# Attention's output projection: seven block products for a pair of tiles, weights loaded in pieces, page numbers read from on-chip memory

## The chip, the cores and the metric

The kernel runs on one core of one Trainium2 chip. Its time is device microseconds (us) of one execution, and the median of several runs is given. The engines that appear below are TensorE (PE; its weight loads are shown apart as PEld), VectorE (DVE), ScalarE (ACT), GpSimd (POOL) and SyncE (SP). Each engine runs its own instructions in order and waits for others through semaphores. SP computes nothing here: it issues almost all DMAs. POOL issues the gathers.

## What is computed

Four layers, each a "condition" stage and a feed-forward stage with a residual, over 64 sequences of 32 tokens with 512 features (2048 rows). The change lies in the condition stage of layer 2, paged attention:

```python
q = rope(rmsnorm(x @ Wq.T))            # 32 heads of 128
k = rope(rmsnorm(x @ Wk.T)); v = x @ Wv.T   # 8 heads of 128
kc = k_cache[block_table].reshape(bsz, L, HK, D)   # 16 pages of 32 keys a sequence
vc = v_cache[block_table].reshape(bsz, L, HK, D)
scores = einsum('bqhd,bkhd->bhqk', q, concat(kc, k)) * SCALE   # masked by cache_seqlens
o = einsum('bhqk,bkhd->bqhd', softmax(scores), concat(vc, v))
return einsum('bse,de->bsd', o.reshape(bsz, seqlen, HQ * D), Wo)   # 4096 -> 512
```

The last line, the product with Wo, is what is computed in another way. Everything is float32.

## The kernel before

The 2048 rows are 16 tiles of 128 rows (four sequences each). Layers 0 and 1 run first, then `attention`, then the `Tail` (layer 2's feed-forward and layer 3).

Attention goes through `steps`: two halves of the heads (16 query heads and 4 key heads each), and in each half the 16 tiles, so 32 steps. A step has 16 turns (4 sequences x 4 key heads). A turn transposes the probabilities of its own scores (L635, `prT_ps`), starts the scores of two turns later (L791 on PE, then L796 to L803 on DVE and ACT) and multiplies values (L640, `po`). Between these, each turn has two places for other work, its "slots" (32 in a step): the projections of the next step (`Projection.product`, in halves of 2 matmuls: `pv`, `pk`, `pq`), their transposes (`turned`), loads and stores, and the output product of the step before (`Output.product`). The order of all PE work is written out by hand and kept by `on_pe`.

The output product of one tile in one half is 16 matmuls, one a head, of a 128x128 block of `oT` (the tile's attention output, heads by rows, transposed) with 128x512 of `wo`, accumulated in one PSUM bank (`py`, L640). A float32 matmul stands in the trace as two instructions, so 32 steps x 16 heads give the 1024 instructions of the profile. `wo` is one resident tile of 16x512 floats a partition, loaded in four DMAs of 1 MB at the start of each half (L855). The first half's result goes to DRAM (`y_part`, L774), the second's is added to it (L770) and stored as `y`. The output of the last step has no turns left to lie between: it runs alone at the end of attention, before the tail.

On SP's queue, `load_keys` loads a sequence's 16 key pages as 16 DMAs of 64 KB (L98). Before them `numbers` (L93) reads the 16 page numbers from DRAM into registers of SP, and checks each against bounds. The tile of keys has two buffers (`cp`), so a load waits until PE is done with the scores of the sequence two before. The values are gathered by POOL (L662). POOL also does two operations of each rotation (L694, L695) and its inverse root (L126), which PE's transposes of q and k need. SP, POOL, DVE and ACT each go through their queues in order: what stands behind a waiting instruction waits too.

## Time and profile before

| | |
|---|---|
| median of 3 runs | 3710.6 us (3705.92 to 3713.36) |
| the profiled execution, its own time | 3681.84 us |
| its span, first to last instruction | 3679.8 us |
| PE busy | 3631.7 us (99%) |
| DVE, ACT, POOL busy | 1805.6, 1316.3, 1254.1 us |
| DMA moved | 407.70 MB, mean 111 GB/s |
| granted TensorE clock | 0.999 |

A group's line gives its engine, operation, what it writes and reads, its shape and count, then the busy time and the mean duration of one. Matmuls overlap in the pipeline: one lasts longer than the distance to the next. The distance between starts, read from the timeline, is what a matmul costs a PE that never idles.

### The profile page before, as it was taken

How to read it: one execution, taken by the hardware profiler on the slowest of the kernel's cores; microseconds unless marked ns; L12 is line 12 of the kernel's file. 1: busy time of each engine (PE TensorE's matmuls, PEld its weight loads, DVE VectorE, ACT ScalarE, POOL GpSimd, SP SyncE). 2: the span in 40 equal slices, each digit the busy share in tenths (PEclk: the TensorE clock that was granted, in tenths of full speed). 3: DMA queues.
4: the chain of work that ended last, by engine and by line, in shares of the span. 5: the costliest groups of instructions: out<-in, count | busy, mean ns of one | idle time of the engine just before them, and what ended most of it. 6: DMA issues, size and time to landing. Idle time of an engine off the chain costs nothing.

```text
span 3679.8 us, 62184 instructions
## 1 busy us (share of the span) xinstructions
PE 3631.7 (99%) x18752; PEld 2523.7 (69%) x18752; DVE 1805.6 (49%) x4815; ACT 1316.3 (36%) x3014; POOL 1254.1 (34%) x1265
## 2 busy tenths in 40 slices
PE   8999999999999999999999999999999999999999
PEld 3444788888867776777777776777777777777755
DVE  5452222222236655565556655566555655566423
ACT  1111111111125444444444444444444444444411
POOL 0112100000035444544445444444444444454222
PEclk9999999999999999999999999999999999999999
DMA  5014211111144444344443355544444344444521
GB/s 209 23 35 162 92 44 60 44 47 34 37 141 134 124 122 122 117 116 116 123 122 118 115 184 179 165 132 119 123 123 125 117 123 122 129 120 123 160 68 61
DMA packets 410062, 407.70 MB, mean 111 GB/s; under 512 B 49954, under 2 KB 322338, under 8 KB 409730
## 3 DMA queue, kind: packets, MB, share of 16 engines
q1 hardware_dynamic: 363010, 251.65, 22.5%
q0 software_dynamic: 44416, 147.88, 13.2%
q10 hardware_dynamic: 2304, 4.20, 0.3%
q8 instruction: 153, 2.51, 0.3%
q14 instruction: 179, 1.47, 0.1%
HBM read 382.57 MB, written 20.97 MB: 110 GB/s over the span
## 4 chain that ended last, share of the span: by engine, by line
PE 89%; SPq 1%; DMA 0%; DVE 0%; issue 0%; ACT 0%; POOL 0%; ACTq 0%; POOLq 0%; DVEq 0%
PE po L640 14%; PE sc L791 13%; PE pq L640 12%; PE py L640 12%; PE gate_up L311 10%; PE prT_ps L635 6%; PE pz L311 5%; PE po L1100 3%; PE pv L640 3%; PE pk L640 3%; PE po L311 2%; PE qkT_ps L635 2%; PE pd L247 1%; PE ph L122 1%; SPq L93 0%
## 5 line engine op out<-in xcount | busy, mean ns | idle before, releaser
L662 POOL DMA_INDIRECT vt<-in_v_rows,v_rows x512 | 500.7, 978 | 816.7 <-PE po L640 708.8
L640 PEld LDWEIGHTS po<-prT,vt 128*128 128x128 f32 x4096 | 530.1, 192 | 183.7 <-issue 178.0
L796 DVE CUSTOM_DVE_ANT_0 pr<-sc,mask 128x544 f32<-128x544 f32 x512 | 369.2, 721 | 458.7 <-PE sc L791 457.5
L798 ACT ACTIVATE pr<-pr,low 128x544 f32<-128x544 f32 x512 | 383.4, 749 | 540.7 <-DVE low L796 536.4
L791 PE MATMUL sc<-kt,qT 128*128 128x288 f32 (+1 forms) x2048 | 555.1, 394 | 5.2 <-ACT qT L748 2.4
L640 PE MATMUL po<-prT,vt 128*128 128x128 f32 x4096 | 540.8, 275 | 1.6 <-ACT prT L809 1.6
L791 PEld LDWEIGHTS sc<-kt,qT 128*128 128x128 f32 x2048 | 369.2, 191 | 180.8 <-issue 106.9
L640 PE MATMUL py<-wo,oT 128*128 128x512 f32 x1024 | 480.3, 593 | 0.7 <-ACT oT L839 0.7
L640 PE MATMUL pq<-wq,xT 128*128 128x512 f32 x1024 | 480.9, 593 | 0.0
L809 ACT COPY prT<-prT_ps 128x512 f32<-128x512 f32 x512 | 298.5, 583 | 272.6 <-PE prT_ps L635 269.4
L803 DVE TENSOR_SCALAR pr<-pr,low 128x512 f32<-128x512 f32 x512 | 364.5, 712 | 16.7
L635 PE MATMUL prT_ps<-ident,pr 128*128 128x128 f32 x2048 | 310.9, 275 | 1.3 <-DVE pr L803 1.3
L640 PEld LDWEIGHTS py<-wo,oT 128*128 128x128 f32 x1024 | 192.6, 191 | 137.5 <-issue 125.6
L640 PEld LDWEIGHTS pq<-wq,xT 128*128 128x128 f32 x1024 | 182.8, 191 | 129.9 <-issue 125.1
L800 DVE RECIPROCAL low<-low 128x1 f32<-128x1 f32 x512 | 83.5, 163 | 360.6 <-ACT pr L798 359.6
L635 PEld LDWEIGHTS prT_ps<-ident,pr 128*128 128x128 f32 x2048 | 237.7, 141 | 9.1 <-issue 1.5
L126 POOL TENSOR_TENSOR rs<-rs,minus_half 128x4 f32<-128x4 f32 x160 | 166.2, 1039 | 167.4 <-DVE rs L678 166.1
L694 POOL TENSOR_TENSOR rot<-rot,swapped 128x512 f32<-128x512 f32 x160 | 202.7, 1267 | 1.0
L801 ACT ACTIVATE own_pr<-pr,low 128x32 f32<-128x32 f32 x512 | 164.2, 321 | 106.3 <-DVE low L800 104.2
L695 POOL TENSOR_TENSOR rot<-rot,rs 128x512 f32<-128x512 f32 x160 | 177.1, 1107 | 8.0
L395 DVE TENSOR_TENSOR sg<-sg,gate_up 128x256 f32<-128x256 f32 (+1 forms) x88 | 37.1, 421 | 277.3 <-ACT sg L394 277.3
L677 DVE TENSOR_REDUCE rs<-squares 128x4 f32<-128x512 f32 x160 | 109.6, 685 | 118.9 <-ACT squares L675 116.3
(208 smaller groups left out, 4649.8 us busy)
## 6 DMA issues: line engine op xcount, KB each, us to landing
kt<-in_kT SPq DMA_DIRECT2D x2048, 64.0 KB
xt<-x SPq DMA_DIRECT2D x48, 256.0 KB
wq<-in_WqT SPq DMA_DIRECT2D x12, 1024.0 KB
A<-in_A SPq DMA_DIRECT2D x64, 152.0 KB
sets<-in_cond0T SPq DMA_DIRECT2D x32, 256.0 KB
vt<-in_v_rows,v_rows POOLq DMA_INDIRECT x512, 3.7
wo<-in_WoT SPq DMA_DIRECT2D x8, 1024.0 KB
y<-y SPq DMA_DIRECT2D x32, 256.0 KB
```

The lines of the kernel that those rows point to most:

```text
L126: self.nc.gpsimd.tensor_tensor(t, t, self.minus_half[:, :n], ALU.pow)
L311: c.on_pe(nc.tensor.matmul(out, lhsT, rhs, start=start, stop=stop))
L635: c.on_pe(nc.tensor.transpose(pt[:, m, :], piece, c.ident))
L640: c.on_pe(nc.tensor.matmul(out, lhsT, rhs, start=first and i == 0, stop=last and i == len(pairs) - 1))
L662: nc.gpsimd.indirect_dma_start(out=vts[b % 2][:, n, :], out_offset=None, in_=a["v_rows"], in_offset=bass.IndirectOffsetOnAxis(ap=rows[h][: ...
L694: nc.gpsimd.tensor_tensor(r, r, tmp, ALU.add)
L695: last = nc.gpsimd.tensor_tensor(r, r, rs.unsqueeze(2).to_broadcast([P, REP, HD]), ALU.mult)
L791: c.on_pe(nc.tensor.matmul(sc[:, lo + n * PSIZE:lo + m * PSIZE].rearrange("p (n k) -> p n k", k=PSIZE), q, kt[:, n:m, g, :], start=True, s ...
L796: nc.vector.tensor_tensor_reduce(pr[:, :NK], sc[:, lo:lo + NK], masks[h, b], -SCALE, 3.0e38, ALU.add, ALU.min, low[:, 0:1])
L798: nc.scalar.activation(pr[:, :NK], pr[:, :NK], AF.Exp, bias=low[:, 0:1], scale=-1.0, accum_out=low[:, 1:2])
L803: nc.vector.tensor_scalar(pr[:, :L], pr[:, :L], low[:, 2:3], None, ALU.mult)
L809: nc.scalar.copy(prT, pt)
```

## The change

The output of two tiles (steps 2n and 2n+1, the "pair" n) in one half is now one product of a 256x2048 matrix with a 2048x512 matrix. It is cut into 2x2 blocks (rows: the two tiles; inner: the first 8 and the last 8 heads; columns: the first and the last 256), and computed as seven products of blocks in place of eight, with sums of blocks before and after (Winograd's form of Strassen's method):

- `first_sums` (on POOL, for the last pair on DVE) and `next_sum` (DVE) add and subtract blocks of `oT`, partly in place, partly in a new tile `o_sum`. `oT` has three buffers, not two.
- `sum_up` makes the four sums of blocks of Wo, once for each half: 16 times in steps 0 and 1 it loads two 256 KB pieces of Wo, makes four 128x256 sums on DVE, and stores 512 KB to a new DRAM tensor `wo_sums`.
- Each block product is 8 matmuls (one a head) with 256 columns, in two halves of 4. `wo` is no longer resident: a piece of 512 KB (4 heads x 256 columns, rows of 1 KB), from Wo or from `wo_sums`, is loaded for each half product, with four buffers. The next piece is issued by SP one slot after a half product.
- Results are put together by ACT (copies of products 1 and 5), DVE (adds from PSUM) and POOL (two adds of 256 columns; in the second half two adds of `y_before`).
- The slots of projections and outputs are laid out anew for even and odd steps. A pair's 14 half products take 8 slots in the next even step and 6 in the next odd one; the last pair's 14 run alone at the end.
- The page numbers are loaded once into an on-chip tile `pages`, held between the bounds by DVE, and SP reads them from there, without checks.
- All of `load_by`'s DMAs (key pages, wo pieces, sums) are issued in the order of the text. A sequence's 16 page loads are given out in four parts: the first where it was, the others in the next slots, at most two such items a slot.

The core of the diff:

```diff
     def load_by(self, dst, src):
-        self.last_load = self.nc.sync.dma_start(dst, src).ins
+        with self.tc.issue_after(self.last_load) if self.last_load else nullcontext():
+            self.last_load = self.nc.sync.dma_start(dst, src).ins
...
+        def load_keys(h, b, parts=range(4)):
+            if 0 in parts:
+                pages[:] = c.numbers(
+                    known.pages[b:b + 1, :], PAGES,
+                    skip_runtime_bounds_check_because="Known holds them between the bounds")
+            for n in range(parts[0] * NPP // 4, (parts[-1] + 1) * NPP // 4):
+                c.load_by(kts[h, b][:, n, :], a["kT"][ds(pages[n], 1), h].rearrange("a d f -> (a d) f"))
...
+        H = D // 2
+        KH = HQP // 2
+        QH = KH // 2
+        ORDER = (1, 2, 5, 6, 7, 3, 4)
+        ahead = 4
+        def wo_tile():
+            return op.tile([P, QH, H], F32, name="wo", bufs=ahead)
+        def sum_up(h, k):
+            w, t = [], []
+            def rows():
+                w.append(wo_tile())
+                for n in range(2):
+                    at = (h * HQP + n * KH + k) * HD
+                    c.load_by(w[0][:, 2 * n:2 * n + 2, :].rearrange("p a b -> p (a b)"),
+                              a["WoT"][at:at + HD, :])
+            def add():
+                t.append(wo_tile())
+                (b11, b12, b21, b22), (t1, t2, t3, t4) = ([v[0][:, n, :] for n in range(4)] for v in (w, t))
+                nc.vector.tensor_tensor(t1, b12, b11, ALU.subtract)
...
+            def store():
+                c.load_by(sums[h][:, k], t[0])
...
+            def first_sums(self, engine):
+                self.o = [oTs.pop(2 * self.n + i) for i in range(2)]
+                (_, _), (o21, o22) = self.blocks = [(o[:, :KH, :], o[:, KH:, :]) for o in self.o]
+                self.s = qp.tile([P, KH, P], F32, name="o_sum", bufs=1)
+                engine.tensor_tensor(self.s, o21, o22, ALU.add)
+                engine.tensor_tensor(o21, self.blocks[0][0], o21, ALU.subtract)
...
+            def product(self, i):
+                m, u = ORDER[i // 2], i % 2
...
+                    self.acc = ps.tile([P, D], F32, tag="mm", bufs=2, name="py")[:, :H]
+                (o11, o12), (o13, o22) = self.blocks
+                lhs = {1: o11, 2: o12, 3: self.s, 4: o22, 5: self.s, 6: self.s, 7: o13}[m]
+                w = wos.pop(0)
+                part(self.acc, [(lhs[:, u * QH + n, :], w[:, n, :]) for n in range(QH)], u == 0, u == 1)
...
-                load_keys(h, b)
+                load_keys(h, b, range(1))
+                later.extend(partial(load_keys, h, b, range(n, n + 1)) for n in range(1, 4))
...
+                    ats = (18, 19, 21, 23, 25, 27, 29, 31) + tuple(2 * per + at for at in (1, 2, 4, 5, 7, 8))
...
+                        slots[at].append(partial(out.product, i))
+                        slots[at].append(partial(later.append, next_wo))
...
+        out = outputs[-1]
+        out.befores()
+        out.first_sums(nc.vector)
+        for i in range(n_out):
+            out.product(i)
+            next_wo()
+            if i in (5, 7):
+                for u in range(2):
+                    out.next_sum(6 if i == 5 else 3, u)
```

## The prediction

> **What bounds the kernel now.** I read the page's busy table and chain of waits first, to see whether one engine sets the end.

> ```profile
> span 3679.8 us, 62184 instructions
> PE 3631.7 (99%) x18752; PEld 2523.7 (69%) x18752; DVE 1805.6 (49%) x4815; ACT 1316.3 (36%) x3014; POOL 1254.1 (34%) x1265
> PEclk9999999999999999999999999999999999999999
> PE 89%; SPq 1%; DMA 0%; DVE 0%; issue 0%; ACT 0%; POOL 0%; ACTq 0%; POOLq 0%; DVEq 0%
> ```

> PE is busy 99% of the span at full granted clock, and 89% of the chain that ended last is PE's. So time follows what PE must do, unless a change makes PE wait. A busy PE may still hold bubbles, so next I read its timeline for the distance between starts, once in attention, once in layer 1, and at the end of attention.

> ```profile
> 2042.42 1.88 PE L640 MATMUL py<-wo,oT 128*128 128x512 f32 x4
> 2044.14 1.05 PE L640 MATMUL po<-prT,vt 128*128 128x128 f32 x8
> ...
> 900.46 1.89 PE L311 MATMUL gate_up<-xT,gate1T 128*128 128x256 f32 x8
> 902.19 0.60 PE L311 MATMUL gate_up<-low_x,Bg 128*128 128x256 f32 x2
> 902.62 1.89 PE L311 MATMUL gate_up<-xT,up1T 128*128 128x256 f32 x8
> ...
> 3495.25 14.00 PE L640 MATMUL py<-wo,oT 128*128 128x512 f32 x32 [0.67 <-ACT oT L839]
> 3510.03 0.66 PE L1117 MATMUL yT_ps<-ident,y 128*128 128x128 f32 x4 [0.79 <-DVE y L770]
> ```

> Columns: start, length, line, what, count, wait before. Four `py` of 512 columns take 2044.14 - 2042.42 = 1.72 us, 0.430 us each. Ten matmuls of 256 columns in layer 1 take 902.62 - 900.46 = 2.16 us, 0.216 us each: half the columns, half the distance. The last two lines show one output alone at the end, with small waits at both sides.

> Then PE's waits inside attention (from 1081 us to 3495 us), SP's waits, and the stretches of attention with most DMA:

> ```profile
> PE sc L791 <- ACT qT L748: 2.4, 3, 1.0
> PE sc L791 <- DMA kt<-in_kT: 1.6, 1, 1.6
> ...
> SPq L98 <- PE sc L791: 215.0, 72, 5.2
> ...
> 1081.80:1160.00 78.20, 74.08 (x410) 54.08 (x411) 52.13 (x134) 39.48 (x94) 49.41 (x54) 1.00 0.57 175
> 1160.00:1238.00 78.00, 78.00 (x412) 55.30 (x411) 45.73 (x120) 37.18 (x86) 34.59 (x36) 1.00 0.46 133
> 2178.00:2255.00 77.00, 76.96 (x400) 53.97 (x399) 45.31 (x120) 35.55 (x82) 34.89 (x36) 1.00 0.60 194
> 2255.00:2333.00 78.00, 76.27 (x397) 53.52 (x397) 44.34 (x117) 35.55 (x82) 34.36 (x36) 1.00 0.52 162
> ```

> PE waits 8.1 us in all of attention (six kinds, the two longest shown). SP waits 215 us for PE before loads of keys: the queue is early, not late. In the stretches the columns are length, PE, PEld, DVE, ACT and POOL busy, clock, DMA share, GB/s. Even at 194 GB/s and a share of 0.60 PE is busy 76.96 of 77 us; the next stretch loses 1.7 us.

> **The change part by part.**

> *Fewer products (PE).* Before: 32 steps x 16 heads x 2 instructions = 1024 x 0.430 = 440.3 us. After: 32 tile-halves make 16 pairs; each has 7 products x 8 heads x 2 = 112 instructions of 256 columns, 1792 x 0.216 = 387.1 us. All lies on the bounding engine: **-53.2 us**. Weight loads rise from 1024 to 1792; `py`'s last 191 ns each, under the 216 ns between matmuls, and layer 1's `gate_up` loads weights for each of its matmuls too at that pace. Cost 0. The scores' 256-column form would give the same price.

> [...]

> *Sums of Wo in steps 0 and 1.* 16 x 4 = 64 subtractions of 256 columns on DVE at 0.42 us (layer 1's 128x256 tensor-tensor): 27 us in about 151 us (a step is (3495.25 - 1081.77)/32 = 75.4 us). DVE is busy 52 of 78 us and 46 of 78 there, so it rises to about 0.8: hidden by DVE's idle time, but a sum that waits for its rows holds the softmax of a later turn behind it, and PE needs that two turns (9.4 us) on. DMA: 16 x (0.52 + 0.52) = 16.8 MB more, less the 4.2 MB of resident `wo`. Step 0 goes from 175 to about 175 + 111 - 54 = 232 GB/s, step 1 from 133 to 244. With 194 GB/s at share 0.60 (323 GB/s if full), that is a share of 0.72 to 0.76. No row shows attention at this rate. Lower bound 0, indeed -1.6 us (the wait for `kt` could go). Upper: both steps lose what the 162 GB/s stretch lost, scaled by extra traffic to some 8 us a step, 15 us. It is nearest to the 194 GB/s row, which lost nothing: **+2 us**.

> *Pieces of Wo.* 14 a pair, 7.3 MB in 151 us: +49 GB/s, so 129 becomes about 178, below the 194 of the row above; SP pays 7 more issues a step at about 0.52 us (16 key pages take 8.3 us). A piece waits on SP until PE has finished the half product four before. Behind it on SP stand key pages, `xt`, stores; for these wait the scores. But the piece is issued a slot after that product was due, and is needed some 8 slots (8 x 2.36 = 19 us) later. If SP's lead were gone, keys would be next late. SP also gets time back: a sequence's page numbers cost it loads of 0.86 and 1.82 us and 16 checks of 0.17 us, 5.4 us, against one load on chip; a lead that was not needed, so worth 0 to 1.6 us. The page loads in parts come up to two slots later, 4.7 us, against SP's wait of 3.0 us a time and five turns until use. Value 0, bounds -1.6 and +8 (PE's present waits in attention doubled).

> *Sums and adds of outputs.* DVE per pair: before 2 x 0.69, after 5 x 0.42 + 4 x 0.69, +3.5 us in 151; ACT two copies more. POOL: two sums of 1024 columns, by L694's 1.27 us for 512 some 5 us together, and up to 3.8 us of adds. POOL waits for `oT`'s last copies; behind it stand gathers and the rotations that PE transposes five slots (11.8 us) after the projection. DVE idles 42%, POOL 55%: hidden. If it were not, each pair would lose at most the excess of a late rotation, say half a microsecond (PE waits for ACT or DVE today are 0.3 to 1.0 us each), 8 us. Value **+1 us**.

> *The end.* The last pair's 14 half products run alone: 112 x 0.216 = 24.2 us, counted above. The wait of 0.67 for `oT` goes, since product 1 reads the earlier tile. A new one comes between products 5 and 6, where `o_sum` is changed in place: one DVE operation of 512 columns, 0.69 + 0.1, like the 0.79 of the timeline: **+0.1 us** net. Four pieces are there, ten follow at one a 1.73 us: 303 GB/s. Neither the 209 GB/s of the page's first slice nor 323 settles it: 5.24 MB at 209 GB/s take 25.1 us against 17.3, so 0 to 7.8 us. I take **+2 us**, nearer to 323, as the queue then carries little else.

> [...] The profile shows no landing time for 512 KB. [...]

> *Sum.* -53.2 + 2 + 0 + 1 + 0.1 + 2 = **-48.1 us**. The profiled execution took 3681.84 (2.0 around its span), so it would take 3633.7. The median shown is 28.8 us above the profiled one; I carry that over whole: 3710.6 - 48.1 = **3662.5 us**.

> **The rivals.**

> *A: the gain is half eaten by transfers.* All upper bounds come true: steps 0 and 1 15, pieces 8, sums 8, end 7.8: -53.2 + 38.8 = -14.4, 3696; with half of them, 3677. For it: 0.52 and 0.60 shares already cost 1.7 us. Against: SP's 215 us of lead. I set it at 3690.

> *B: slower, by late pieces.* Place: SP's queue, where a piece stands behind key pages that wait for PE up to 5.2 us, and four buffers. If the piece comes after its product is due, PE waits at each of 224 half products. It decides from 53.2/224 = 0.24 us a piece; with the 0.4 us in the middle of PE's present waits it is 90 us, 3747. Against: 19 us of distance; 194 GB/s without loss.

> *C: it does not do what it says.* At 0.246 us a matmul (as the scores' 288-column form has: four `sc` in 0.92 us, less two at 0.216) 1792 cost as much as 1024 did: 3710. Against: every 256-column row has 0.216.

> **How the numbers follow.** Forecast 75%, A 12%, B 9%, C 4%. The forecast alone spans -55 to -40 us and some 4 us between runs: 3652 to 3675. The range reaches through most of A: 3650 to 3697. 0.2% (7.4 us) is about what a measurement can tell from no change. Faster: 0.75 + 0.12 = 0.87; within: C, 0.04; slower: B, 0.09.

> **What would show it.** `py` in 1792 instructions of 256 columns 0.216 us apart; PE still 98 to 99% busy, in a span near 3632; waits of PE for `wo` near 0 before the end and a few us there; steps 0 and 1 near 230 to 245 GB/s with PE full; SP still waiting for PE. Wrong: PE waits for `wo`, `kt` or `rot` in the tens of us, or another distance between `py`.

## The result: slower, by 1.4% in the first comparison

| comparison | kernel before, us | changed kernel, us | ratio, 95% interval |
|---|---|---|---|
| the first | 3711.98 (3705.92 to 3714.83, 4 runs) | 3764.08 (3757.46 to 3768.67, 4 runs) | 1.0141 [1.0119, 1.0163] |
| second, run e5 | 3684.26 | 3698.01 | 1.0033 [1.0019, 1.0048] |
| third, run e11 | 3680.34 | 3700.97 | 1.0051 [1.0034, 1.0068] |
| fourth, run e13 | 3712.72 | 3765.45 | 1.0140 [1.0122, 1.0157] |

The comparisons are of two kinds whatever the kernel: in some the kernel before takes about 3711 us, in others about 3682, and the profile of before that the prediction read (3681.84 us) is of the second kind, while the timed runs shown with it are of the first. I call them the 3711 and the 3682 comparisons. The prediction was 48 us faster, so about 100 us have to be found in the first kind and 62 to 69 in the second.

The page of the changed kernel's first profile (3760.5 us for the execution): the span, the busy times, the granted clock, and the shares of the chain that ended last.

```profile
span 3758.7 us, 60219 instructions
PE 3618.2 (96%) x19520; PEld 2678.1 (71%) x19520; DVE 1896.8 (50%) x4996; ACT 1307.7 (35%) x3046; POOL 1377.4 (37%) x1343
PEclk9999999999999999999999999999999999999999
PE 84%; DMA 4%; POOL 4%; issue 2%; DVE 2%; SPq 1%; ACT 1%; another core or an unknown queue 1%; DVEq 0%; ACTq 0%; POOLq 0%
```

PE is busy 13.5 us less than before (3631.7), where 53 less were forecast, and it idles 140 us of the span in place of 48. Part of what it is busy longer is clock: the mean over the span is 0.990, against 0.999, too fine for the line in tenths. The clock's records show 15 stretches at half speed, 12 of them in attention; the profile of before had 3, none of them there. What PE waits for:

```profile
PE po L652 <- ACT prT L905: 51.4, 17, 3.5
PE qkT_ps L647 <- POOL rot L711: 14.0, 15, 1.1
...
PE sc L887 <- DVE low L892: 7.4, 5, 4.6
PE pk L652 <- DMA wk<-in_WkT: 6.8, 1, 6.8
...
PE py L652 <- DMA wo<-wo_sums: 4.0, 3, 1.7
PE pq L652 <- DMA wq<-in_WqT: 3.6, 1, 3.6
```

And the longest of the waits of SP's queue:

```profile
SPq L100 <- PE sc L887: 764.4, 118, 12.1
```

None of the waits is the one that rival B named: `py` waits 4.0 us for pieces of `wo` in all. SP waits 764 us for PE before loads of keys (215 before), so its lead has grown. The longest wait, 51.4 us, is for ACT's copy of `prT`, 17 times at up to 3.5 us; 13 of them, 44.6 us, stand at the first turn of a pair of steps, and two more such turns wait 2.7 and 2.0 us with "issue" as the cause. Before the change all of attention had 8.1 us of waits.

To see where the time goes I cut attention into its 16 pairs of steps, by the starts of the first transposes of `prT` in the timeline (the last pair reaches to the first `yT_ps`). "Forecast" is the kernel before (run e15) with what the products alone move: 13.74 us out of pair 0, 3.29 out of each other pair, and 7.16 into the last.

| pairs, us | before, e15 | forecast | after, first | after, e5 | best, e10 |
|---|---|---|---|---|---|
| 0 (steps 0, 1) | 143.6 | 129.8 | 151.3 | 149.3 | 141.0 |
| 1 to 6, 8 to 14, each | 151.66 | 148.37 | 152.8 to 157.0 | 150.2 to 151.0 | 149.0 to 149.4 |
| 7 (change of halves) | 153.4 | 150.1 | 169.9 | 171.2 | 149.0 |
| 15 and the last output | 151.9 | 159.1 | 169.3 | 165.0 | 161.6 |

Over the forecast the first profile loses 21.5 us in pair 0, 82.7 in the 13 steady pairs, 19.8 at the change of halves and 10.2 at the end. In e5 the same four are 19.5, 24.8, 21.1 and 5.9: three lie within 5 us of the first profile's, and the steady pairs are what differs between the two kinds of comparison.

### The profile page after: what moved, and what is told of

Read it like the earlier page. It is cut to its first block, busy times and chain, and to the rows that moved or that the text cites. A ratio compares the mean times of both kernels' runs of the same rounds, so it can differ in the third digit from the quotient of the medians.

```text
span 3758.7 us, 60219 instructions
## 1 busy us (share of the span) xinstructions
PE 3618.2 (96%) x19520; PEld 2678.1 (71%) x19520; DVE 1896.8 (50%) x4996; ACT 1307.7 (35%) x3046; POOL 1377.4 (37%) x1343
## 4 chain that ended last, share of the span: by engine, by line
PE 84%; DMA 4%; POOL 4%; issue 2%; DVE 2%; SPq 1%; ACT 1%; another core or an unknown queue 1%; DVEq 0%; ACTq 0%; POOLq 0%
PE po L652 13%; PE sc L887 10%; PE gate_up L313 10%; PE pq L652 10%; PE py L652 10%; PE prT_ps L647 5%; PE pz L313 4%; PE po L1237 3%; PE ph L124 3%; PE pk L652 2%; PE pd L249 2%; PE pv L652 2%; PE po L313 2%; PE qkT_ps L647 2%; DMA wo<-in_WoT 1%
## 5 line engine op out<-in xcount | busy, mean ns | idle before, releaser
L652 PE MATMUL po<-prT,vt 128*128 128x128 f32 x4096 | 553.3, 279 | 57.5 <-ACT prT L905 51.4
L652 PE MATMUL py<-wo,oT 128*128 128x256 f32 x1024 | 241.9, 380 | 4.0 <-DMA wo<-wo_sums 4.0
L652 PE MATMUL py<-wo,o_sum 128*128 128x256 f32 x768 | 181.0, 379 | 0.1
```

Of the source, the lines that this page charges most:

```text
L652: c.on_pe(nc.tensor.matmul(out, lhsT, rhs, start=first and i == 0, stop=last and i == len(pairs) - 1))
```

## The experiments

Each kernel is the changed one with the edit shown, unless another is named. Each was timed beside the kernel before.

### Is it the program or the occasion?

Five runs without an edit: the kernel before (e1, e15) and the changed one (e5, e11, e13).

> The kernel before, unchanged, profiled once more. Its first profile (3681.84 us, clock 0.999) lies 29 us under its timed runs (3705.92 to 3713.36); the changed kernel's profile (3760.5) lies among its timed runs. Theory: an execution of the kernel before takes about 3710 us as a rule and loses the 29 us to stretches of granted clock below 1.0 that the first profile did not catch: this profile then shows a span near 3705 and a clock near 0.992. Rival: the profile of before is always near 3682 and only unprofiled executions are longer: span 3680, clock 0.999.

> The changed kernel, unchanged, once more. The wait for ACT's copy of prT (51.4 us in its first profile) is 1.9 us or less in three variants of it, of which two (page numbers from DRAM, first sums on DVE) don't touch the work between scores and values at the turn where it stood. Theory 1 (it belongs to this program's order): the wait is here again, 45 to 55 us with a clock near 0.990, and the time stands 1.2 to 1.6% over the kernel before. Theory 3 (it belongs to the execution of that day, as the 29 us of the kernel before did): the wait is under 10 us, the clock 0.995 or more, the time within 0.3% of the variant with the first sums on DVE, 0.2 to 0.8% over the kernel before.

> The changed kernel, unchanged, a third time, to see on which chips the wait of 51.4 us for ACT's copy of prT stands. Where the kernel before takes about 3684 us I expect what the last run of it showed: steady pairs of 150.2 us, a wait for prT under 2 us, 1.0033 of the kernel before. Where the kernel before takes about 3710 us I expect the wait of 51 us, steady pairs of 153.5 to 156.5 us and 1.014.

Measured: e1 3681.64 us, 0.9996 [0.9987, 1.0006] of the runs beside it, span 3688.8, clock 0.997. Neither theory's numbers; the kernel before simply takes 3682 us there, profiled or not. e5 and e11 took 1.0033 and 1.0051 and had no wait for `prT` to speak of (1.5 us in e5). So the wait of 51.4 us isn't this program's order alone.

The first turn of an even step on PE, in the first profile of the changed kernel and then in e5 (start, length, line, what, count, wait before):

```profile
2013.34 0.66 PE L647 MATMUL prT_ps<-ident,pr 128*128 128x128 f32 x4
2013.83 1.08 PE L887 MATMUL sc<-kt,qT 128*128 128x288 f32 x4
2018.32 1.44 PE L652 MATMUL po<-prT,vt 128*128 128x128 f32 x5 [3.41 <-ACT prT L905]
```

```profile
1989.49 0.66 PE L647 MATMUL prT_ps<-ident,pr 128*128 128x128 f32 x4
1989.98 1.08 PE L887 MATMUL sc<-kt,qT 128*128 128x288 f32 x4
1991.19 1.16 PE L652 MATMUL po<-prT,vt 128*128 128x128 f32 x8
```

And ACT at the same places:

```profile
2014.80 0.59 ACT L935 COPY oT<-po 128x512 f32<-128x512 f32 x1 [0.77 <-PE prT_ps L647]
2017.68 0.59 ACT L905 COPY prT<-prT_ps 128x512 f32<-128x512 f32 x1 [2.30 <-remote]
```

```profile
1990.08 0.57 ACT L935 COPY oT<-po 128x512 f32<-128x512 f32 x1
1990.55 0.59 ACT L905 COPY prT<-prT_ps 128x512 f32<-128x512 f32 x1
```

In e5 the two copies follow the transposes at once. In the first profile ACT is idle and the transposes have long been issued, yet the copy starts 4.3 us after they did: PE's signal came late. The trace's signal records show it for all of PE: 267 signals lie 0.12 us or more behind the modelled end of their instruction in the first profile, 36 in e5 and 36 in the kernel before in e15. These 36 lie outside attention, 34 of them at 0.12 us; inside attention there are 231 in the first profile and none in e5 and e15. At the first turn of even steps the copy of `prT` starts 3.69 us behind the end of its transposes in the median, against 0.41 in e5, where the copy of `oT` stands between. The late signals bunch where the batch's own values have just been multiplied and POOL gathers the next rows, at turns 0 and 16 of a pair above all (139 of the 231). The work itself is no slower: in the mean the copy of `prT` takes 0.58 us, a gather 0.98 to 0.99 and a packet of 1 KB 51 ns in both profiles.

### The first turn of even steps, covered

```diff
-                    plan = (("v", 2, 3), ("k", 4, 5), (0, 6, 7), ...
+                    plan = (("v", 1, 2), ("k", 4, 5), (0, 6, 7), ...
```

> The changed kernel with one edit: in even steps the product of v starts at slot 1 (slots 1 and 2, as before the change) in place of slots 2 and 3, so that 1.72 us of PE work lie between the scores and the values of the step's first turn. Theory 1 (an uncovered turn): the changed kernel waits there 51.4 us for ACT's copy of prT, 17 times, and each such gap is followed by 3.4 us or more at half the granted clock, because nothing lies between prT's transposes and its use. The wait then falls from 51.4 to under 15 us, the low clock in attention from 15 events to about 5, the time by 50 to 75 us, to 3690 to 3715. Theory 2 (a late signal): ACT starts that copy up to 3.7 us after PE's transposes whatever PE does next, since something else holds PE's signals up; then the wait only shrinks by the 1.7 us of the new cover, 17 times, to about 22 us, and the time to about 3720 to 3735.

> The changed kernel with v's product at slots 1 and 2 of even steps, again. Where the kernel before takes about 3684 us: the first turn of even steps loses 0.4 us without the cover (steps of 76.30 against 75.91), so 6 us less than the changed kernel of this call. Where the kernel before takes about 3710 us: theory 1 (the uncovered turn is what the slower chip punishes) gives 50 to 75 us less than the changed kernel of this call; theory 2 (signals are late there whatever PE does) gives at most 30 us less.

> The changed kernel with v's product at slots 1 and 2 of even steps. If the kernel before takes about 3712 us beside it: the wait for prT falls from 51 to 57 us to 25 to 30, the low clock of the steady pairs goes, and the time is 1.002 to 1.005 of the kernel before, as in the earlier comparisons (3715 to 3730 us against 3764). If the kernel before takes about 3682 us: 1.002 to 1.004, no such waits.

Measured: 3691.88, 3692.84 and 3690.87 us, ratios 1.0025 [1.0015, 1.0034], 1.0030 [1.0018, 1.0043] and 1.0021 [1.0011, 1.0030]. All three fell into 3682 comparisons, where there is no long wait to remove. Even steps take 75.91 us in place of 76.30, 0.4 us each, and against e11, timed beside e12, it is 8.1 us. That confirms the small expectation alone. In the first profile half the clock followed 9 of the 14 waits for `prT` of over 3.3 us, not each, as the first expectation says.

### Page numbers from DRAM, first sums on DVE

```diff
-                    known.pages[b:b + 1, :], PAGES,
-                    skip_runtime_bounds_check_because="Known holds them between the bounds")
+                    a["pages"][0:1, b * NPP:(b + 1) * NPP], PAGES)
```

> The changed kernel with one edit: SP reads a sequence's page numbers from DRAM and checks each, as before the change (two loads of 0.84 and 1.8 to 2.4 us and 16 checks), in place of one load of 1.0 us from an on-chip tile. Theory 2a (the on-chip reads hold PE's signals up): the lag between prT's transposes and ACT's copy at the first turn of even steps falls from a median of 3.69 us to under 0.3, the wait of 51.4 us with it, and the time to about 3700. Theory 1 (an uncovered turn) and every other: lag and wait stay, the time is 3764 within 10 us; only SP's lead gets smaller by 4.4 us a sequence.

```diff
-                    slots[4].append(partial(out.first_sums, nc.gpsimd))
+                    slots[4].append(partial(out.first_sums, nc.vector))
```

> The changed kernel with one edit: the two first sums of a pair's outputs (two of 1024 columns, 2.35 us each on POOL) run on DVE in place of POOL. Theory 2b (POOL's long sums hold up PE's signals, DVE's scaling of the softmax and the rotations behind them): the lag at the first turn of even steps and the 14.0 us of waits for rot fall by more than half, the time by 20 to 60 us. Theory 1 (an uncovered turn): the 51.4 us for ACT's copy stay within 5 us, since POOL's sums start after the gap has begun (2017.06 against 2014.9 us); the sums then queue on DVE ahead of a softmax, and the time is 3764 within 10 us or a little longer.

Measured: e3 3868.26 us, 1.0507 [1.0489, 1.0524]; e4 3700.38, 1.0052 [1.0036, 1.0069]. In neither is the wait for `prT` there, since it isn't in e5 either: they tell nothing of its cause. e4 stands where e5 and e11 do, so moving POOL's two sums of 2.35 us away gains nothing, and the wait for `rot` is still 14.0 us: it isn't theirs. e3 is a finding of its own. Its waits on PE:

```profile
PE py L652 <- DMA wo<-wo_sums: 105.1, 25, 7.4
PE sc L886 <- DVE low L891: 18.2, 6, 8.8
...
PE sc L886 <- DMA kt<-in_kT: 6.9, 5, 2.2
```

In e3 the two loads take 1.49 and 2.02 us and the 16 checks start 0.25 us apart, 7.5 us a sequence against one load of 1.00. With 6.5 us more a sequence SP loses its lead (it waits 81 us for PE before loads of keys, in place of 764), pieces come late, and each of the 18 waits of 5 us or more in attention is followed by half the clock (27 stretches of it in the whole program). This is rival B, and the part of the change that I had put at 0 to 1.6 us is what keeps it away: about 170 us (3868 against 3698 to 3701).

### The weights at the change of halves

```diff
-                if steps[s + 2][0] != h:
+                if steps[s + 2][0] != steps[s + 1][0]:
```

> The changed kernel with one edit: at the change of halves the weights of v, k and q are loaded in step 14 alone. As written (and in the kernel before too) step 15 loads the same weights again. Theory: the second load does harm only since the change, because products of an odd step now begin at slot 9 with k, behind the second load (slots 4 to 17), where they began at slot 1 with v before it. Then the waits for wk and wq (6.8 and 3.6 us) go, 12.6 MB less are moved, steps 14 and 15 take 152 to 157 us in place of 169.9, and the time falls by 10 to 16 us against the changed kernel of this call. Rival: the waits come from the first load, made late by SP's queue of pieces: then only the bytes go and the time stays within 4 us.

Measured: 3678.44 us, 0.9984 [0.9974, 0.9993]; pair 7 takes 150.2 us in place of 171.2, and the waits for `wk` and `wq` are gone. The gain, 20 us, is larger than expected since the half clock after the waits goes too (10.24 us from 2273.90 on in the changed kernel's first profile). Step 15 of the changed kernel's first profile:

```profile
2270.42 1.08 PE L887 MATMUL sc<-kt,qT 128*128 128x288 f32 x4
2278.32 3.78 PE L652 MATMUL pk<-wk,xT 128*128 128x512 f32 x4 [6.82 <-DMA wk<-in_WkT]
2281.89 1.91 PE L652 MATMUL po<-prT,vt 128*128 128x128 f32 x8
...
2284.30 1.88 PE L652 MATMUL pk<-wk,xT 128*128 128x512 f32 x4
2286.02 1.08 PE L887 MATMUL sc<-kt,qT 128*128 128x288 f32 x4
...
2299.47 0.70 PE L652 MATMUL pq<-wq,xT 128*128 128x512 f32 x1 [3.62 <-DMA wq<-in_WqT]
```

SP issues that `wk` at 2267.84, 3.5 us before PE would have come to it. After the wait four `pk` take 3.57 us (2278.32 to 2281.89), the next four 1.72 (2284.30 to 2286.02): half speed. The condition in the code holds for steps 14 and 15, so the same weights are loaded twice; before the change the second load ran behind step 15's products, now it stands ahead of them.

### Three edits together, and the sums on POOL

The cover, the weights once, and the last transposes of an odd step one slot later:

```diff
-                    then = zip(("k",) + GROUPS, (13, 17, 20, 24, 27))
+                    then = zip(("k",) + GROUPS, (13, 17, 20, 24, 28))
```

> The changed kernel with three edits: v's product covers the first turn of even steps, weights are loaded once at the change of halves, and the transposes of group 3's q in odd steps move from slot 27 to 28. Steady pairs of steps took 149.8 us with the cover alone, 151.66 in the kernel before, and 148.4 would be the products' saving in full (151.66 less 112 x 0.216 against 64 x 0.430, 3.3 us). The third edit should take away the 1.1 us wait for rot in each pair: steady pairs at 148.7, 14 x 1.1 = 15 us; with the second some 12 us more. Theory: 3692 - 15 - 12 = about 3665, 0.4 to 0.6% faster than the kernel before. Rival: the wait for rot only moves to the next slot (a later scores instruction waits for qT): steady pairs stay at 149.8 and the time near 3680.

Measured: 3664.07 us, 0.9957 [0.9943, 0.9971], as expected to 1 us. Steady pairs take 149.04 us, the wait for `rot` is gone; 0.2 us a pair come back as a wait of `xT_ps` for ACT. So this faster kernel is the changed one with products and transposes at other slots and one load of weights less.

The same kernel with the subtractions for the sums of Wo on the other engine, all four of them like this one:

```diff
-                nc.vector.tensor_tensor(t1, b12, b11, ALU.subtract)
+                nc.gpsimd.tensor_tensor(t1, b12, b11, ALU.subtract)
```

> The kernel of the run before in this call (cover, weights once, later transposes) with the 64 subtractions for the sums of Wo in steps 0 and 1 on POOL in place of DVE. Steps 0 and 1 hold 13.7 us less product work than before the change, yet took 151.3 us against 143.6 to 147.6: about 20 us are lost there, more than any other part of the change. Theory: DVE is what is late there, since four subtractions of 0.34 to 1.8 us stand ahead of a softmax that PE needs two turns on; on POOL they hold up nothing that PE needs and steps 0 and 1 take 130 to 140 us. Rival: the rows of Wo come late through SP's queue and the turns without other work are bound by the chain scores, softmax, transposes in any case; then steps 0 and 1 stay at 145 to 150 us, or grow as rotations on POOL wait behind the sums.

Measured: 3673.06 us, 0.9969 [0.9959, 0.9980]; pair 0 takes 156.3 us against 147.1. The rival's second half: on POOL a subtraction takes 0.73 us (0.42 on DVE) and PE waits up to 7.0 us for `rot` behind them. The theory fell in this form: the work has to go, not to another engine.

### Half the sums later, pieces ahead of pages

The kernel of e7, with the second half's sums moved:

```diff
-                for k in range(KH):
-                    for f, at in zip(sum_up(s, k), (0, 5, 7)):
-                        slots[min(3 * k + at, 2 * per - 1)].append(f)
+                for k in range(4 * s, 4 * s + 4):
+                    for f, at in zip(sum_up(0, k), (0, 5, 7)):
+                        slots[min(7 * (k % 4) + at, 2 * per - 1)].append(f)
...
+                    if n <= 4:
+                        for k in range(2):
+                            for f, at in zip(sum_up(1, 2 * (n - 1) + k), (10, 17, 19)):
+                                slots[at + 10 * k].append(f)
```

The first four pieces of pairs 1 to 5 are then issued at slots 8 to 14 of the even step.

> The kernel with cover, weights once and later transposes (3664.07 us, 0.9957), with the sums of Wo's first half spread over steps 0 and 1 (one head every seven slots in place of one every three) and those of the second half moved to steps 3, 5, 7 and 9, two heads each, in the slots where no output is made. Steps 0 and 1 took 147.1 us there; 143.57 less 13.74 of product work that has moved out is 129.8. Theory (DVE's subtractions stand ahead of the softmax in turns that have no other work on PE): half the sums, half the loss, steps 0 and 1 at 136 to 141 us, the four odd steps each within 1 us of 73.1, the time 5 to 11 us shorter, about 3656. Rival (such turns are bound by scores, softmax and transposes in any case): steps 0 and 1 stay above 144 us and the odd steps grow: the time is the same or longer.

Measured: 3655.64 us, 0.9934 [0.9917, 0.9950]; pair 0 takes 139.7 us and the odd steps 73.1 to 73.4. As the theory had it: with half the sums 7.4 of the 17.3 us that pair 0 lost went. How such a loss arises stands in the changed kernel's first profile, on PE and then on DVE:

```profile
1135.01 0.60 PE L647 MATMUL prT_ps<-ident,pr 128*128 128x128 f32 x4
1140.16 1.72 PE L887 MATMUL sc<-kt,qT 128*128 128x288 f32 x4 [4.55 <-DVE low L892]
```

```profile
1134.39 0.42 DVE L795 TENSOR_TENSOR wo<-wo 128x256 f32<-128x256 f32 x1
1134.73 0.68 DVE L935 COPY oT<-po 128x512 f32<-128x512 f32 x1
1135.33 0.42 DVE L796 TENSOR_TENSOR wo<-wo 128x256 f32<-128x256 f32 x1
1135.78 1.16 DVE L685 COPY own_vt<-v 32x128 f32<-32x128 f32 x5
1137.12 0.42 DVE L793 TENSOR_TENSOR wo<-wo 128x256 f32<-128x256 f32 x1 [0.18 <-DMA wo_sums<-wo]
...
1139.39 0.71 DVE L892 CUSTOM_DVE_ANT_0 pr<-sc,mask 128x544 f32<-128x544 f32 x1
```

PE stands from 1135.61 until the softmax at 1139.39 has read the last scores. Ahead of that softmax DVE works through sums, copies and a rotation almost without a pause (0.18 us).

Then one more edit, the order in which SP gets a due piece:

```diff
-                            slots[at].append(partial(later.append, next_wo))
+                            slots[at].append(partial(later.insert, 0, next_wo))
```

> The kernel of the run before in this call, with one more edit: a piece of Wo that has become due goes ahead of the deferred parts of a sequence's page loads in SP's order, in place of behind them. In the last pair of steps a piece was issued at 3412.96 us for a product due at 3414.1, behind 16 page loads of 0.52 us that waited for PE's scores, and PE lost 6.3 and 1.6 us there, and 3.6 at half the clock. Theory (pieces behind page loads, my rival B, real in the last pair alone): steps 30 and 31 go from 167.8 to 158 to 162 us and the time falls by 5 to 10 us. Rival (the buffers are what is late, or the pages come late in their turn): the last pair stays above 166 us, or PE waits for kt in the steady pairs and the time is longer.

Measured: 3649.78 us, 0.9919 [0.9902, 0.9935], the fastest; pair 15 takes 161.6 us against 167.9. In e7 the piece was behind pages (SP's queue, then PE):

```profile
3396.41 1.93 SPq L100 DMA_DIRECT2D wo<-wo_sums  x2
3399.68 13.18 SPq L100 DMA_DIRECT2D kt<-in_kT  x16
3412.96 0.38 SPq L100 DMA_DIRECT2D wo<-wo_sums  x1
```

```profile
3420.58 3.44 PE L652 MATMUL py<-wo,oT 128*128 128x256 f32 x8 [6.09 <-DMA wo<-wo_sums]
```

### The late signals once more

> The changed kernel, unchanged, a fourth time, in another session. If the kernel before takes about 3711 us here: the late signals are the chip's, and I expect over 200 of them, 45 to 55 us of waits for prT and 1.012 to 1.016 of the kernel before. If the kernel before takes about 3682 us: under 50 late signals, no such wait, 1.003 to 1.006.

> The kernel with cover, weights once, later transposes, half the sums later and pieces ahead of page loads, again (0.9919 before). Where the kernel before takes about 3682 us: 0.990 to 0.994. Where it takes about 3711 us: if the late signals cost what PE has nothing else to do for, the cover holds most of it off and the ratio is 0.99 to 1.00; if they cost in every turn, 1.00 to 1.01.

Measured: a 3711 comparison. The changed kernel has 274 late signals, 57.3 us of waits for `prT`, 15 stretches of half clock and 1.0140 [1.0122, 1.0157]; the first result is reproduced. e10's kernel takes 3682.44 us, 0.9917 [0.9900, 0.9933]: its gain holds in both kinds. It has 276 late signals, so the lateness is not a thing of the first changed order alone; but v's product covers half of it. In e13 the first turns of the pairs wait 3.4 us each, in e14, from pair 2 on, 1.7 to 1.8, with the copy as late (3.7 us) in both:

```profile
1987.05 1.88 PE L652 MATMUL pv<-wv,xT 128*128 128x512 f32 x4
1990.69 0.49 PE L652 MATMUL po<-prT,vt 128*128 128x128 f32 x2 [1.76 <-ACT prT L905]
```

Its steady pairs take 151.03 us there against 149.04 in e10, 2.0 us more, with no half clock in them; the whole kernel takes 32.7 us more, and its waits for `prT` are 28.3 us in place of 1.5.

The chip doesn't decide it alone: the chip numbered 15 ran e5 to e8, where the kernel before took 3684 us, and also e13, e14, e17 and e18, where it took 3709 to 3713.

For a profile of the kernel before under this condition it and the cover (e16 above) ran once more:

> The kernel before, unchanged. If it takes about 3712 us here: its trace has over 200 late signals and PE waits 1.5 to 2 us for ACT's copy of prT at the first turn of every second step, some 25 to 30 us in all, with few stretches of low clock, since v's product (1.72 us) covers the rest of the 3.5 us. If it takes about 3682 us: under 50 late signals and 1.6 us of such waits.

Measured: 3681.64 us, 1.0000 [0.9991, 1.0010], 36 late signals: the condition wasn't there. So the copy was made late by hand, in both kernels (line of the changed one):

```diff
-            nc.scalar.copy(prT, pt)
+            for _ in range(7 if i and i % (2 * SEQ * HKP) == 0 else 1):
+                nc.scalar.copy(prT, pt)
```

> The kernel before, with ACT's copy of prT made seven times in place of once at the first turn of each even step but the first (15 turns): the values there can start 6 x 0.586 = 3.5 us later, as the late signals make it (lag of 3.69 us). Theory 1 (the cover decides): v's first product (1.72 us) lies between, so PE waits 1.5 to 1.9 us at 15 turns, 22 to 29 us, with no more low clock than without: 3704 to 3712 where the kernel before takes 3682, ratio 1.006 to 1.008. Rival (ACT's lateness costs the same in either order, because the softmax behind it is late as well): 50 us and more, 1.014 or over.

> The changed kernel with the same: seven copies of prT in place of one at the first turn of each even step but the first. Theory 1 (the cover decides): nothing lies between, so PE waits 3.2 to 3.8 us at 15 turns, 48 to 57 us, and the longer gap is followed by half the granted clock in some of them, 1.7 to 3.7 us each, so that steady pairs take 153.5 to 156.5 us and the time is 3750 to 3775 where the changed kernel takes 3699: 1.018 to 1.025 of the kernel before. Rival: the loss is that of the other kernel, steady pairs near 152 and 3725 us.

Measured: e17 3817.17 us, 1.0297 [1.0280, 1.0314]; e18 3854.36, 1.0389 [1.0372, 1.0407]. Both missed, for two reasons. This was a 3711 comparison: 295 and 268 signals were late already, and the copies came on top. And six copies cost more than 3.5 us, because ACT had softmax work between them. One such turn of e17, on PE and then on ACT, and one of e18 on PE:

```profile
1876.95 1.88 PE L640 MATMUL pv<-wv,xT 128*128 128x512 f32 x4
1883.96 2.08 PE L640 MATMUL po<-prT,vt 128*128 128x128 f32 x8 [5.12 <-ACT prT L810]
```

```profile
1878.43 1.82 ACT L810 COPY prT<-prT_ps 128x512 f32<-128x512 f32 x3 [1.59 <-PE sc L791]
1880.66 0.75 ACT L798 ACTIVATE pr<-pr,low 128x544 f32<-128x544 f32 x1 [0.42 <-DVE low L796]
1881.32 0.19 ACT L798 ACTIVATION_READ_ACCUMULATOR pr<-pr,low 128x1 f32 x1
1881.41 0.56 ACT L810 COPY prT<-prT_ps 128x512 f32<-128x512 f32 x1
1881.88 0.32 ACT L801 ACTIVATE own_pr<-pr,low 128x32 f32<-128x32 f32 x1
1882.10 1.80 ACT L810 COPY prT<-prT_ps 128x512 f32<-128x512 f32 x3
```

```profile
2041.57 1.08 PE L887 MATMUL sc<-kt,qT 128*128 128x288 f32 x4
2049.70 2.07 PE L652 MATMUL po<-prT,vt 128*128 128x128 f32 x8 [7.04 <-ACT prT L906]
```

From the start of the first copy to the end of the seventh it takes 5.5 us here (4.96 to 6.88 over the 15 turns), against 0.59 for one copy. By the timeline's starts PE stands 5.2 to 5.3 us at most of these turns in e17 (1883.96 less 1876.95 and 1.72 for `pv`; 3.8 at two, 6.2 at one) and 7.0 to 8.5 in e18. Not all of that difference is the cover, since the first copy isn't equally late: the median lag is 2.2 us in e17 and 3.7 in e18. But two turns of e18 have the lag (2.24 and 2.27 us) and the copies (5.46 and 5.48 us) of e17's usual turn (2.23 and 5.47): there PE stands 7.0 us against 5.3. The 1.7 us between them are v's product.

The added copies cost the kernel before more (3817 - 3709 = 108 us) than the changed one (3854 - 3765 of e13 = 89). The kernel before had next to no half clock without them (none in attention in its first profile and in e15, two stretches in e1) and has 18 stretches in attention in e17; the changed kernel had 12 in e13 and has 22 in e18.

What these runs don't show is the kernel before under late signals without the copies. With a lag of 2.2 us and one copy, v's product would leave 0.4 us of wait at such a turn, as it does at the one turn of e14 with this lag (2.23 us, pair 1): too little for the 29 us by which 3711 differs from 3682.

## Why the prediction was wrong, by its steps

- **Fewer products, -53.2 us: right.** Eight `py` take 0.216 us each from start to start, as forecast; in a steady pair `py` takes 24.18 us in place of 27.47. The 1792 weight loads, 190 ns each, cost nothing beside these 0.216; rival C is out.
- **Sums of Wo in steps 0 and 1, +2 (bounds -1.6 to 15): pair 0 loses 19.5 to 21.5, outside the bounds.** I took DVE's mean share, 0.8, as cover, and two mean turns of 9.4 us as the time until PE needs the softmax. But pair 0 makes no outputs any more: turns of 4.0 to 5.8 us early in step 1 become as short as 2.4, as some of step 0 were before, a softmax stands behind subtractions, and PE has nothing else to do meanwhile. Half the sums are worth 7.4 us of it (e9); how the rest divides isn't shown. The traffic I feared came (204 and 224 GB/s in steps 0 and 1, against 232 and 244 forecast) and was hardly what PE waited for (1.6 us in all for rows of Wo).
- **Pieces, page reading, split page loads, 0 (bounds -1.6 to 8).** Right for the steady pairs. In the last pair a piece behind pages cost 6.3 us (e10). The page reading wasn't worth 1.6 us at most but about 170 (e3): the pieces need the lead that it gives. Its 5.4 us of SP's time was low as well, since the checks start 0.25 us apart and not 0.17, which makes 6.7.
- **Sums and adds of outputs, +1.** Moving POOL's sums gains nothing (e4). The late rotation that I put at 0.5 us a pair is 1.1, but it comes from the slots, and one slot later it is gone (e7).
- **The end, +0.1 and +2: right.** From the first of the last 112 `py` to `yT_ps` it takes 25.3 to 26.2 us in four traces, 1.2 to 2.0 over 112 x 0.216.
- **Not priced at all: the projections' new slots.** This is the step that failed most. The prediction has no term for them, although the diff moves v's product off the first turn of even steps and the products of odd steps behind slot 9. The first costs 0.4 us a pair where signals come on time. Where they are late, PE stands 3.6 us at such a turn (e13) in place of the 1.8 to 1.9 that e14 shows with the cover, and half the clock follows in 14 of 24: the changed kernel takes some 65 us more in the one kind of comparison than in the other, e10's kernel 33 and the kernel before 29. The second put step 15's products behind a second load of weights that had always been there: 21 us.
- **The base.** I made the sum on a profile 29 us under the median and carried that over whole. That profile and the timed runs were of different kinds. What the kernel before loses in the 3711 kind was never in a profile; e10's kernel, with the same cover, loses about as much, most of it in waits for `prT`. That the kernel before does the same is likely and not shown.

By the pairs it adds up: in e5 the forecast's -52.6 and the four losses, 19.5 + 24.8 + 21.1 + 5.9, give +18.7, and -0.6 ahead of attention +18.1; its span is 3697.07 against 3678.98 in e15. Edits against all four (e10) give 0.992 in both kinds of comparison, still 21.7 us short of the forecast over the pairs: 11.2 in pair 0, 9.1 in the steady pairs, 2.5 at the end, less 1.1 in pair 7. What they are isn't shown.

Two things stay open. What makes PE's signals late isn't known: the runs show when (some comparisons, any kernel) and where, and that engines and DMAs are no slower. And the cover by itself was never run under that condition; that it halves the wait there rests on e14, which has four other edits too, and on the matching turns of e17 and e18.

## What to carry to other kernels

When a change takes work off the engine that bounds, list the places where that work, or any that is moved to make room, lay between a producer and its consumer; what it covered must be priced by the turn, not by an engine's mean share. A load that was issued twice cost nothing here while it ran behind its users (no wait for `wk` or `wq` in the kernel before), and 10.4 us of waits when they moved: look in the queue for repeats before shifting products. And compare the profiled execution with the timed runs: a gap of 0.8% between them meant that they were taken under different conditions, and the profile couldn't show what the other condition makes PE wait for.
